# Pairs of a symmetric attention as (i, i + k) mod 128 instead of triangular blocks, with the leaky rectifier in ScalarE's evacuation and the scores put back into rows through DRAM

## The chip, the cores and the metric

One core of one Trainium2 chip. The metric is the device time of one execution in microseconds (us); a kernel's figure is the median of its runs. PE is TensorE, DVE is VectorE, ACT is ScalarE, POOL is GpSimd; hp, ps, d, z and so on are the names of the kernel's tiles: d holds the differences of a tile of pairs, hp their product with W1 (two halves of 64 rows, each a matmul of its own), z the hidden layer behind the leaky rectifier (max(h, 0.01 h), "the leaky" below), ps the scores, lnrs the inverse roots of a layer norm.

## The reference

Four graph layers are applied to 128 batches of 128 tokens with 128 features, all in fp32, each with a layer norm and a maximum with 0 ahead of it and a residual sum behind it. Layer 0 is a relational sum over seven relations. Layers 2 and 3 are plain attention and stay as they were. The change is about layer 1, whose scores come from all pairs of tokens:

```python
D = jnp.abs(x[:, :, None, :] - x[:, None, :, :])        # [128, 128, 128, 128]
h = jnp.einsum('bijc,oc->bijo', D, W1) + b1             # 64 outputs per pair
m = jnp.mean(h, axis=(0, 1, 2))                         # batch norm over every pair of every batch
v = jnp.mean((h - m) ** 2, axis=(0, 1, 2))
h = (h - m) / jnp.sqrt(v + EPS) * g1 + be1
h = _leaky(h)                                           # max(h, 0.01 h)
s = jnp.einsum('bijo,uo->biju', h, W2)[..., 0] + b2[0]
s = jnp.where(A_init > 0, s, NEG)
A = jax.nn.softmax(s, axis=-1)
y = jnp.einsum('bij,bjc->bic', A, x)
# ... linear layer, second batch norm, leaky, concatenation, linear layer
```

D is symmetric, so about half of the pairs suffice. The batch norm needs statistics of all pairs of all batches before any score can be made. The pairs are therefore worked out twice, and the kernel has three stages:

- A: layer 0, woven with the pairs' statistics.
- B: the pairs again, scores, softmax and product of layer 1.
- C: the rest of layer 1, then layers 2 and 3.

## The kernel before

The symmetric half is cut into triangular blocks: block I has rows 16 I to 16 I + 15 and the columns from 16 I on. Five tiles of pairs make a batch.

```python
PAIR_TILES = [(0,), (4,), (2, 6), (1, 7), (3, 5)]
ON_POOL = {(3, 5)}                      # the tile whose differences GpSimd makes
...
def pairwise(pool, xT, blocks):
    n = sum(8 * (P - 16 * I) for I in blocks)
    d = pool.tile([P, 2, 1024], F32, tag="d", bufs=3, name="d")
    ...
    for I in blocks:
        ...
        eng = nc.gpsimd if blocks in ON_POOL else nc.vector
        eng.tensor_tensor(o, <columns of xT>, <rows of xT>, OP.subtract)             # L183
    nc.scalar.activation(d[:, :, :n], d[:, :, :n], AF.Abs)                           # L187
    hp = big("hp").rearrange("p a b -> p (a b)")
    for c in range(0, n, 512):
        for hh in range(2):                                                          # two halves of 64 rows
            nc.tensor.matmul(hp[64 * hh:64 * hh + 64, c:c + 512], w1T,
                             d[:, hh, c:c + 512], start=True, stop=True)             # L191
    return hp, n, places
...
def scores(hT, ps):                                                                  # stage B
    nc.tensor.matmul(ps, ones[0:1, :], b2row, start=True, stop=False, ...)
    for blocks in PAIR_TILES:
        hp, n, places = pairwise(p1, hT, blocks)
        z = p1.tile([P, 1024], F32, name="z")
        nc.scalar.activation(z[:, :n], hp[:, :n], AF.Identity, bias=bias1, scale=scale1[:, 0:1])   # L341
        nc.vector.scalar_tensor_tensor(z[:, :n], z[:, :n], 0.01, z[:, :n],
                                       op0=OP.mult, op1=OP.max)                      # L342, the leaky
        for I, w, off in places:
            for r in range(8):                                                       # 64 small matmuls a batch
                nc.tensor.matmul(ps[q:q + 32, 16 * I:P], w2z[:, s:s + 32],
                                 z[:, off + r * w:off + (r + 1) * w], ...)           # L347
        yield
```

Layer norms take their inverse roots from GpSimd (L136 and L137, tile lnrs), in the same queue as its tile of differences. The input x of all groups of four batches is kept on chip.

## Time and profile before

The median was 7855.92 us (three runs, 7853.16 to 7866.12).

| stage of before | length, us | PE busy | DVE busy | ACT busy |
|---|---|---|---|---|
| A, layer 0 and statistics | 3329 | 69% | 87% | 38% |
| B, scores and softmax | 3081 | 88% | 77% | 61% |
| C, layers 2 and 3 | 1423 | 65% | 64% | 28% |

A stage runs from its own first instruction to the first one of what follows; the batch norms between the stages (some 15 us and 3 us) are in none of them, so that the stretches of the profile lines differ from the table by up to 3 us. Busy shares overlap: in A the DVE is the fullest engine, in B it is PE. The lines themselves stand in the prediction below.

### The profile page before, as it was taken

The numbers are of one execution on the slowest core, as the hardware profiler recorded it, in microseconds if no ns is written. First come the engines' busy times: TensorE is split into PE (matmuls) and PEld (weight loads), VectorE is DVE, ScalarE is ACT, GpSimd is POOL, SyncE is SP. The second block draws the span as 40 slices with busy tenths as digits, with TensorE's granted clock in tenths as the row PEclk, the third lists the DMA queues.
The fourth block names the chain that finished last, engine by engine and source line by source line (L and its number), as shares of the span: only waits on it lengthen the run. The fifth ranks groups of instructions, "written<-read, shape, count | busy, mean of one in ns | idle before, by whom it ended". The sixth has DMA issues, their size and how long they took to land.

```text
span 7851.8 us, 90855 instructions
## 1 busy us (share of the span) xinstructions
PE 5922.0 (75%) x36100; PEld 3189.2 (41%) x36100; DVE 6192.1 (79%) x10853; ACT 3545.3 (45%) x3489; POOL 1368.8 (17%) x884
## 2 busy tenths in 40 slices
PE   6676766777666676688888888888888876666666
PEld 3222222222222222244444444444444445555555
DVE  7888888888888888877777777777777766666666
ACT  2333333333333333355666666666666642222222
POOL 1222222122222222111111111111111210000000
PEclk8777777777777777799999999999999996667666
DMA  2000000000000000000000000000000000000000
GB/s 56 3 3 2 3 3 3 3 3 3 3 3 3 3 2 1 1 1 1 1 1 1 1 1 1 1 1 1 1 1 1 1 2 6 6 9 6 6 6 9
DMA packets 55639, 32.19 MB, mean 4 GB/s; under 512 B 3762, under 2 KB 55218, under 8 KB 55218
## 3 DMA queue, kind: packets, MB, share of 16 engines
q1 hardware_dynamic: 38322, 18.00, 0.9%
q10 hardware_dynamic: 16896, 8.39, 0.3%
q8 instruction: 287, 4.70, 0.2%
q14 instruction: 134, 1.10, 0.0%
HBM read 18.00 MB, written 8.39 MB: 3 GB/s over the span
## 4 chain that ended last, share of the span: by engine, by line
PE 52%; DVE 32%; POOL 7%; ACT 7%; issue 1%; SPq 0%; DMA 0%; POOLq 0%; ACTq 0%; DVEq 0%
PE hp L191 23%; PE ps L347 10%; DVE d L183 9%; ACT d L187 6%; POOL d L183 5%; DVE st_o L210 4%; DVE hn L149 3%; PE pa L264 3%; PE pv L475 3%; PE pa L267 2%; PE ph L258 2%; PE pt L166 2%; DVE z L342 2%; DVE st_d L205 2%; POOL lnrs L137 1%
## 5 line engine op out<-in xcount | busy, mean ns | idle before, releaser
L191 PE MATMUL hp<-d,w1T 128*64 128x512 f32 x9216 | 2906.4, 688 | 854.3 <-ACT d L187 853.2
L187 ACT ACTIVATE d<-d 128x2048 f32<-128x2048 f32 (+1 forms) x1280 | 2192.3, 1734 | 1732.2 <-DVE d L183 1122.9
L183 DVE TENSOR_TENSOR d<-h 128x2048 f32<-128x2048 f32 (+5 forms) x1536 | 2422.0, 1582 | 295.6 <-PE hp L191 295.6
L183 POOL TENSOR_TENSOR d<-h 128x1280 f32<-128x1280 f32 (+1 forms) x512 | 1103.5, 2176 | 4129.6 <-PE hp L191 4118.4
L191 PEld LDWEIGHTS hp<-d,w1T 128*64 128x64 f32 x9216 | 709.0, 151 | 2380.9 <-ACT d L187 1273.0
L347 PE MATMUL ps<-z,w2z 128*32 128x128 f32 (+3 forms) x16384 | 1104.5, 233 | 167.8 <-DVE z L342 167.6
L347 PEld LDWEIGHTS ps<-z,w2z 128*32 128x32 f32 x16384 | 974.8, 112 | 606.3 <-DVE z L342 246.6
L342 DVE SCALAR_TENSOR_TENSOR z<-z 128x1024 f32<-128x1024 f32 (+1 forms) x640 | 963.8, 1511 | 315.7 <-ACT z L341 306.6
L341 ACT ACTIVATE z<-hp,bias,scale 128x1024 f32<-128x1024 f32 (+1 forms) x640 | 714.9, 1117 | 561.9 <-PE hp L191 542.6
L210 DVE BATCH_NORM_STATS2 st_o<-hp 128x6 f32<-128x384 f32 (+5 forms) x1280 | 642.2, 523 | 0.0
L264 PE MATMUL pa<-hw,mask 128*128 128x128 f32 x1792 | 320.6, 320 | 235.2 <-DVE mask L252 184.6
L264 PEld LDWEIGHTS pa<-hw,mask 128*128 128x128 f32 x1792 | 255.8, 214 | 562.8 <-ACT d L187 241.9
L260 ACT COPY hw<-ph 128x384 f32<-128x384 f32 (+1 forms) x256 | 136.3, 533 | 737.1 <-PE ph L258 737.1
L205 DVE BATCH_NORM_STATS2 st_d<-hp 128x6 f32<-128x128 f32 x1024 | 290.6, 289 | 165.0 <-PE hp L191 164.6
L166 PE MATMUL pt<-ident,hn 128*128 128x128 f32 x512 | 138.1, 408 | 367.5 <-DVE hn L160 303.3
L136 POOL TENSOR_SCALAR lnrs<-lnmv 128x4 f32<-128x4 f32 x128 | 30.7, 240 | 1918.2 <-DVE lnmv L144 1918.2
L273 DVE SCALAR_TENSOR_TENSOR o<-pa,rdeg,o 128x128 f32<-128x128 f32 x896 | 300.1, 338 | 11.0 <-PE pa L264 7.1
L166 PE MATMUL pt<-ident,e 128*128 128x128 f32 x640 | 129.0, 355 | 233.2 <-ACT e L459 233.2
L166 PEld LDWEIGHTS pt<-ident,hn 128*128 128x128 f32 x512 | 84.8, 201 | 510.6 <-issue 247.1
L258 PE MATMUL ph<-relw,h 128*128 128x384 f32 (+1 forms) x512 | 283.4, 640 | 0.0
L252 DVE TENSOR_TENSOR mask<-adjT,rel 128x896 f32<-128x896 f32 x128 | 169.5, 1324 | 88.6 <-PE pa L264 88.5
L475 PEld LDWEIGHTS pv<-wr,eT 128*128 128x128 f32 x1280 | 229.6, 280 | 0.0
(143 smaller groups left out, 5161.5 us busy)
## 6 DMA issues: line engine op xcount, KB each, us to landing
x<-in_x_dram SPq DMA_DIRECT2D x32, 256.0 KB, 5.4
adj<-in_adj_dram SPq DMA_DIRECT2D x32, 256.0 KB, 2.8
out_dram<-x ACTq DMA_DIRECT2D x32, 256.0 KB, 2.3
relw<-in_rel_w_dram SPq DMA_DIRECT2D x1, 448.0 KB, 4.3
w<-in_W_dram SPq DMA_DIRECT2D x2, 64.0 KB, 2.1
wgT<-in_WgT_dram SPq DMA_DIRECT2D x1, 64.0 KB, 1.7
wtxT<-in_WtT_dram SPq DMA_DIRECT2D x1, 64.0 KB, 1.8
bt<-in_bt_dram SPq DMA_DIRECT2D x1, 64.0 KB, 3.0
```

Of the source, the lines that this page charges most:

```text
L166: nc.tensor.transpose(pt[:, k, :], src[:, k, :], ident)
L183: eng.tensor_tensor(o, xT[:, None, None, 16 * I:P].to_broadcast([P, 2, 8, w]), rows[:, :, :, None].to_broadcast([P, 2, 8, w]), OP.subtract)
L187: nc.scalar.activation(d[:, :, :n], d[:, :, :n], AF.Abs)
L191: nc.tensor.matmul(hp[64 * hh:64 * hh + 64, c:c + 512], w1T, d[:, hh, c:c + 512], start=True, stop=True)
L205: nc.vector.bn_stats(st_d[:, nd, :], v[:, :, 0:16])
L210: nc.vector.bn_stats(st_o[:, no, :], v[:, r:r + step, 16:])
L258: nc.tensor.matmul(ph[:, 0:r1 - r0, :], hT[:, k, :], relw[:, r0:r1, :], start=True, stop=True)
L264: nc.tensor.matmul(pa[:, r - r0, :], mask[:, r, :], hw[:, r - r0, :], start=True, stop=True)
L341: nc.scalar.activation(z[:, :n], hp[:, :n], AF.Identity, bias=bias1, scale=scale1[:, 0:1])
L342: nc.vector.scalar_tensor_tensor(z[:, :n], z[:, :n], 0.01, z[:, :n], op0=OP.mult, op1=OP.max)
L347: nc.tensor.matmul(ps[q:q + 32, 16 * I:P], w2z[:, s:s + 32], z[:, off + r * w:off + (r + 1) * w], start=False, stop=I % 2 == 1 and r == 7, ...
L475: nc.tensor.matmul(pv[:, k, 0:n], eTs[t][:, k, :], values[t][k], start=True, stop=True)
```

## The change

Pairs are taken as (i, i + k) mod 128 for k = 1 to 64. All tiles are then alike: four of 2 x 8 x 128 pairs for a batch. Almost every DVE, ACT and PE instruction on the pairs has its full 512, 1024 or 2048 columns (the statistics of a batch's last tile have 384 and 128), and there are 16 hp matmuls a batch in place of 18. The leaky moves into the evacuation on ACT (Prelu with slope 0.01), so DVE loses one instruction per tile. Eight 512-column ps matmuls replace 64 small ones. Scores come out by k; they are picked into columns (pk), stored to DRAM along skewed rows, and loaded back as rows. To pay for the room, x lives in DRAM. GpSimd still makes one tile of differences of each batch, now one of four, and also copies h into the extended tile xe.

The core of the diff (comments, constants and the tail of the softmax are cut):

```diff
-PAIR_TILES = [(0,), (4,), (2, 6), (1, 7), (3, 5)]
-ON_POOL = {(3, 5)}
+KH = 32
+KC = 8
+ROW = P + 2 * KH
+ON_POOL = {1}
...
-    X = [res.tile([P, G, P], F32, tag=f"x{g}", name=f"x{g}") for g in range(NG)]
+    X = [dr.tile([P, G, P], F32, tag=f"x{g}", name=f"x{g}") for g in range(NG)]      # dr is in DRAM
...
-    def pairwise(pool, xT, blocks):
+    def around(pool, hT):
+        xe = pool.tile([P, G, P + 2 * KH], F32, name="xe")
+        nc.gpsimd.tensor_copy(xe[:, :, 0:P], hT)
+        nc.gpsimd.tensor_copy(xe[:, :, P:], hT[:, :, 0:2 * KH])
+        return xe
+
+    def pairwise(pool, xe, k, t):
+        d = pool.tile([P, 2, KC, P], F32, tag="d", bufs=3, name="d")
+        x = xe[:, k, 0:P]
+        ahead = ...                                    # xe from 1 + KC * t on, KC windows in each half
+        eng = nc.gpsimd if t in ON_POOL else nc.vector
+        eng.tensor_tensor(d, ahead, x[:, None, None, :].to_broadcast([P, 2, KC, P]), OP.subtract)
...
-            _weave(pairs(g), layer0(g + 1) if g + 1 < NG else iter(()), 3)
+            _weave(pairs(g), layer0(g + 1) if g + 1 < NG else iter(()), 4)
...
-                nc.scalar.activation(z[:, :n], hp[:, :n], AF.Identity, bias=bias1, scale=scale1[:, 0:1])
-                nc.vector.scalar_tensor_tensor(z[:, :n], z[:, :n], 0.01, z[:, :n], op0=OP.mult, op1=OP.max)
-                for I, w, off in places:               # 64 small matmuls
+                nc.scalar.activation(z, hp, AF.Prelu, bias=bias1, scale=scale1[:, 0:1], alpha=0.01)
+                for c in range(2):
+                    j = 2 * t + c
+                    q, w = 32 * (j % 4), 31 - 2 * (j // 4)
+                    nc.tensor.matmul(ps[q:q + 32, :], w2z[:, w:w + 32], z[:, 512 * c:512 * c + 512],
+                                     start=j < 4, stop=j >= 4, skip_group_check=True)
...
+            nc.sync.dma_start(bass.AP(..., ap=[[ROW + 1, P], [P * ROW, G], [1, 1 + 2 * KH]]), s)
+            u = p1.tile([P, G, ROW], F32, name="u")
+            nc.sync.dma_start(u, rows.rearrange("g i r -> i g r"))
```

## The prediction

> **What bounds the kernel now.** I read first the busy time by stretches, cut where the code changes stage (columns: stretch, its length, then busy us and instruction count of PE, PE weight loads, DVE, ACT and POOL, the granted PE clock, DMA share, GB/s):
>
> ```profile
> 0.00:75.00 75.00, 30.16 (x158) 22.05 (x160) 34.44 (x106) 9.72 (x15) 9.51 (x26) 0.84 0.54 139
> 75.00:3329.00 3254.00, 2261.42 (x9188) 921.53 (x9188) 2858.31 (x5887) 1259.88 (x979) 705.02 (x470) 0.78 0.01 3
> 3344.00:6428.00 3084.00, 2703.19 (x22070) 1492.03 (x22066) 2376.92 (x2455) 1877.47 (x1821) 571.15 (x258) 0.96 0.00 1
> 6428.00:7851.00 1423.00, 921.54 (x4672) 750.71 (x4672) 910.11 (x2379) 393.44 (x672) 82.36 (x128) 0.69 0.02 7
> ```
>
> Stage A (to 3329: layer 0 woven with the pairs' statistics) keeps DVE 88% busy, PE 69% at a clock of 0.78. Stage B (to 6428: layer 1's scores and softmax) keeps PE 88% busy at 0.96, DVE 77%. Stage C (layers 2 and 3) fills nobody. Per batch, A takes 3254/127 = 25.6 us with 22.5 of DVE, B 3084/128 = 24.1 us with 21.1 of PE.
>
> Who waits in A confirms DVE: the first two lines are ACT waiting for DVE and PE for that ACT, while DVE's largest wait for PE is small.
>
> ```profile
> ACT d L187 <- DVE d L183: 1099.2, 319, 8.2
> PE hp L191 <- ACT d L187: 641.8, 229, 8.2
> DVE st_d L205 <- PE hp L191: 164.6, 255, 4.5
> ```
>
> In B, one batch of the chain that ended last shows mostly PE, plus one hole per batch in which the POOL tile is made and then rectified:
>
> ```profile
> 4984.24 1.02 PE hp L191 x2
> ...
> 4985.42 4.21 POOL d L183 x2
> 4989.65 3.72 ACT d L187 x2
> ...
> 4993.41 3.65 PE hp L191 x14
> 4997.06 1.64 PE ps L347 x28
> 4998.70 1.00 PE hp L191 x2
> ```
>
> The durations I use come from the groups kept apart by shape (busy us, mean ns; an fp32 matmul is two instructions):
>
> ```profile
> L187 ACT ACTIVATE d<-d 128x2048 f32<-128x2048 f32 x1024 | 1921.3, 1903 | 1599.4 <-DVE d L183 1070.4 <-POOL d L183 525.1 <-PE hp L191 4.0
> L341 ACT ACTIVATE z<-hp,bias,scale 128x1024 f32<-128x1024 f32 x512 | 615.5, 1202 | 513.0 <-PE hp L191 495.6 <-PE ps L347 17.4
> L183 DVE TENSOR_TENSOR d<-h 128x2048 f32<-128x2048 f32 x256 | 584.3, 2282 | 99.5 <-PE hp L191 99.5
> L183 DVE TENSOR_TENSOR d<-h 128x512 f32<-128x512 f32 x256 | 300.6, 1174 | 0.0
> L210 DVE BATCH_NORM_STATS2 st_o<-hp 128x6 f32<-128x384 f32 x384 | 200.4, 550 | 0.0
> L210 DVE BATCH_NORM_STATS2 st_o<-hp 128x6 f32<-128x512 f32 x128 | 87.4, 683 | 0.0
> ```
>
> **What the Trainium skill says.** (1) "TensorE: Matmul & The Clock Gate", rules for kernel authors, small-M row: outputs in distinct column groups run at the same time. The trace agrees: eight hp instructions (four matmuls, both halves in turn) take 1.92 us on the chain, whereas the two instructions of a single matmul, issued without its partner, take 1.00. (2) "TensorEngine Tiling (Array Packing)", key properties: changing the tiling mode drains the array. hp uses 64 columns, ps 32, so a half left alone before ps matmuls should not overlap them; the 1.00 us above, followed by ps at once, agrees. (3) "ScalarE: Activation LUTs": every function costs the same per element, but another table set costs a reload. Abs and Identity fit one slope here; before has one table load, and the built program after also has just one, so Prelu shares the set with Exp. (4) "SBUF — State Buffer", who interferes with whom: a DVE instruction with two SBUF inputs contends with a GpSimd instruction that reads SBUF. The 512-element d above takes 1174 ns in the mean where other DVE operations of 512 elements take about 690, so it does.
>
> **Stage A, part by part.** Pairs fall from 18 to 16 matmuls and from 9216 to 8192 columns per batch. DVE per batch now: statistics L210 392/78 = 5.0, L205 177.5/78 = 2.3, two aggregates 0.7, in all 8.0 us. After: seven of 512 columns (7 x 0.683 = 4.8), one of 384 (0.55), one of 128 (0.28), aggregates of about 0.5: 6.1. Saved 1.9. Differences on DVE now: 745.7/78 = 9.6 us, of which about 1.2 is waiting for POOL's port (the 512 and 256 forms take 1174 and 886 ns instead of some 690 and 410). After: three of 2048, 6.8 us, and I keep the 1.2: 8.0. Saved 1.5. POOL still makes 2048 columns per batch, plus the copies into xe. So DVE goes from 22.5 to 19.1 us; with the idle 3.1 us per batch kept, a batch takes 22.2, and A becomes 127 x 22.2 + 75 = 2895 us. PE falls by 2/18 of its 11.4 us of hp, so it doesn't become the bound (17.8 - 1.3 = 16.5). The x store and loads are 256 KB each, two buffers deep, and out-transfers of this size land in 2.3 us: hidden.
>
> **Stage B.** DVE loses the leaky operation (630 us in a window of 2000 us that holds 83.3 batches: 7.6 us per batch) and the softmax becomes one instruction per group. DVE after: 3 x 2.28 for d, 0.69 for the copy of ps, 0.4 for the two small ones, and a group's twelve or so 512-column instructions at 0.42 to 0.69 (8.7 us) over four: 10.1 us, from 19. DVE is out of the way. ACT: four Abs of 1.90, four Prelu of 1.20, and 2.5/4 for the rest: 13.0 us, from 15 (614.9 per 1000 us).
>
> PE decides. Now hp is 935.7/83.3 = 11.2 us and ps 719.4/83.3 = 8.6 us. A whole pair of halves costs 2 x 0.427 = 0.85 us (1.92 for two pairs less start-up). I counted in the built order: before, 356 of 1152 pairs are split by other work between the halves; after, 350 of 1020, which is 2.74 per batch. Check on before: (9 + 2.8) x 0.853 + 4.5 starts x 0.15 = 10.8, measured 11.2, ratio 1.04, which fits the clock of 0.96. After: (8 + 2.74) x 0.853 + 5 x 0.15 = 9.9, times 1.04 = 10.3. ps: 64 small matmuls per batch become 8 of 512 columns in four column groups, issued two at a time in 3.75 runs: 3.75 x (0.853 + 0.15) x 1.04 = 3.9, from 8.6. New: four pk products with 16 columns, bound like the 1-column L267 (14 instructions in 1.46 us on the chain), eight instructions, about 1.1 us. Transposes and the linear layers by group: 1.24, from 2.2 with the bias product. Sum 16.6 us, from 21.1.
>
> So PE still bounds B, 3.6 us above ACT. Idle beside PE was 3.0 us per batch, mostly the POOL hole; POOL still makes one 2048-column tile (4.2 us), followed by one Abs instead of two, with a little more room in the ring of three d buffers relative to its tile. I take 1.2 us of idle: 17.8 us, 2278 for the stage. The scores' trip through DRAM (store, load, some 5 us by the 2.3 us landings) comes once a group on DVE, which has 7 us of slack a batch: mostly hidden.
>
> **Stage C.** Same work. x must be loaded; three buffers with two groups in flight means that every second group waits for an out-transfer and a load, about 3 us of which DVE has no other work, x16, and hn with one buffer adds under 1 us x32: 1423 + 60 = 1485.
>
> **Sum.** 2895 + 25 (between stages) + 2278 + 1485 = 6683, I say 6690 us, 0.85 of before.
>
> **Rivals.** (a) The split pairs cost less than a whole pair each, or the POOL hole closes and PE follows ACT: B at 15.5 us, total about 6390. For: ACT alone is 13.0, and the ps column groups could fill beside a lone half. Against: the 1.00 us steps on the chain. (b) New coupling: ACT now has both Abs and Prelu in one strict order with PE, and DVE stands in order behind a DRAM round trip; B at 20 us, total about 6970. For: the hole of 8 us on the chain arises in just this way. Against: ACT and DVE both have slack. (c) In A, PE becomes the bound: its clock is 0.78, and hp ran twice as long in cold stretches; then A gains only PE's 1.3 us: A 3160, total about 6950. Against: DVE hardly waits for PE in A. (d) ACT's Prelu switches table sets against Exp: at 1.3 us a load, twice a group, only 80 us; excluded by the build.
>
> **Range.** B and A are each good to about 200 us, C to 40; together some 300 either way at 8 in 10, with rivals (a) and (b) as the ends: 6380 to 7030. Slower than before by over 2% would need every saving to be eaten by coupling; I give 1%, and 2% for within 2%.
>
> **What would show it.** Right: A near 2900 us with DVE at 85% or more; B near 2280 with PE above 90% busy, hp near 10 and ps near 4 us a batch, ACT near 13; C near 1480 with a wait for the DMA of x. Wrong: PE in B well under 85% busy with ACT or a DMA as its releaser (then rival b), ps not running in parallel, Prelu over 1.2 us, a clock in B under 0.9, or DVE under 80% busy in A.

## The result, and the profile after

The changed kernel took 6773.84 us in the median (four runs, 6772.93 to 6787.43), beside 7854.54 us for the kernel before on the same chip. The ratio is 0.8626, with a 95% interval from 0.8613 to 0.8638. Ratios here are the mean time of one kernel's runs over that of the kernel before in the same rounds, so they are not quite the ratio of the medians.

The total is 1.3% above the predicted 6690 us. The stages show that this closeness owes something to luck:

| stage | before | predicted | after | after minus predicted |
|---|---|---|---|---|
| A | 3329 | 2895 | 3226 | +331 |
| B | 3081 | 2278 | 2113 | -165 |
| C | 1423 | 1485 | 1429 | -56 |

The stretches of A and B in the changed kernel, with the columns that the prediction explains (busy us and instructions of PE, PE weight loads, DVE, ACT and POOL, then the granted PE clock, DMA share, GB/s):

```profile
75.00:3225.00 3150.00, 2188.44 (x8688) 969.34 (x8688) 2427.42 (x4382) 1139.99 (x855) 862.64 (x415) 0.79 0.03 8
3240.00:5353.00 2113.00, 1931.94 (x7986) 611.80 (x7986) 1353.43 (x1307) 1587.21 (x1149) 578.30 (x187) 0.99 0.06 17
```

**A.** DVE's work fell as predicted, from 2858 to 2427 us: 2427 over 127 batches is 19.1 us each. But the stretch shrank by only 104 us. DVE now idles 3150 - 2427 = 723 us, where it idled 3254 - 2858 = 396. The waits of DVE in A say on what, in us in total, times, longest; first the kernel before:

```profile
DVE mask L252 <- PE pa L264: 88.5, 31, 3.3
DVE hn L149 <- POOL lnrs L137: 44.3, 30, 1.5
DVE rdeg L269 <- PE pa L267: 35.0, 61, 2.0
```

and the kernel after:

```profile
DVE st L203 <- PE hp L193: 229.6, 223, 4.7
DVE hn L148 <- POOL lnrs L136: 158.7, 31, 5.2
DVE rdeg L266 <- PE pa L264: 158.1, 124, 2.4
DVE mask L249 <- PE pa L261: 104.7, 62, 2.2
```

Before, the wait for hp was 164.6 us (it is among the prediction's lines). The four growths are 65, 114, 123 and 16 us: 318 of the 327 us of added idle. One is a wait for GpSimd, three are waits for PE.

The chain of waits in A shows what the wait for GpSimd is made of, once a group of four batches (start us, us, what):

```profile
1543.54 4.22 POOL xe L175
1547.76 0.34 POOL xe L176
1548.10 4.15 POOL d L187
1552.27 3.72 ACT d L189 x2
1556.03 6.52 PE hp L193 x16
```

The timeline of DVE over the same time has the other end of it:

```profile
1553.59 1.11 DVE L148 TENSOR_SCALAR hn<-x,lnmv,lnrs 128x128 f32<-128x128 f32 x4 [5.24 <-POOL lnrs L136]
```

The copies into xe and GpSimd's d run first in its queue, and the inverse root of the next group's layer norm stands behind them. DVE, which all of layer 0 goes through, waits 5.24 us for one small instruction, and PE starts its next 16 hp instructions only at 1556. The copy's 4.22 us are not all its own: its mean is 3.94 us in A and 0.68 in B, and here two of DVE's d tiles (4.48 us from 1542.81) run at the same time. So DVE also holds up GpSimd, and then waits for it.

**B.** Groups of B kept apart by shape (busy us, mean ns, then the engine's idle time before them):

```profile
L193 PE MATMUL hp<-d,w1T 128*64 128x512 f32 x4080 | 1218.1, 610 | 1.2 <-ACT d L189 1.2
L187 DVE TENSOR_TENSOR d<-xe 128x2048 f32<-128x2048 f32 x380 | 914.4, 2407 | 478.1 <-PE hp L193 475.5
L372 ACT ACTIVATE z<-hp,bias,scale 128x1024 f32<-128x1024 f32 x512 | 608.4, 1200 | 352.9 <-PE hp L193 352.7
L187 POOL TENSOR_TENSOR d<-xe 128x2048 f32<-128x2048 f32 x127 | 545.5, 4295 | 1275.8 <-PE hp L193 1247.4 <-ACT d L189 28.4
L376 PE MATMUL ps<-z,w2z 128*32 128x512 f32 x2048 | 508.4, 608 | 93.3 <-ACT z L372 93.3
L406 DVE TENSOR_TENSOR u<-u 128x256 f32<-128x256 f32 x32 | 79.6, 2487 | 53.5 <-DMA u<-rows 53.5
```

The Prelu costs 1200 ns, as the Identity of before did (1202). The trip of the scores through DRAM shows as 53.5 us of waiting in the whole stage, and C is 6 us longer with x from DRAM. PE is busy 1932 of 2113 us at a clock of 0.99. Some of what idles it is still GpSimd's tile, as one batch of the chain shows:

```profile
4426.68 4.60 POOL d L187
4431.30 1.92 ACT d L189
```

### The profile page after: what moved, and what is told of

Read it like the earlier page. It is cut to its first block, busy times and chain, and to the rows that moved or that the text cites. A ratio compares the mean times of both kernels' runs of the same rounds, so it can differ in the third digit from the quotient of the medians.

```text
span 6785.6 us, 58156 instructions
## 1 busy us (share of the span) xinstructions
PE 5091.2 (75%) x21510; PEld 2364.6 (35%) x21510; DVE 4731.7 (70%) x8187; ACT 3135.1 (46%) x2690; POOL 1536.1 (23%) x754
## 4 chain that ended last, share of the span: by engine, by line
PE 45%; DVE 30%; POOL 11%; ACT 9%; issue 4%; DMA 0%; SPq 0%; POOLq 0%; DVEq 0%; ACTq 0%
PE hp L193 20%; DVE d L187 9%; POOL d L187 6%; ACT d L189 5%; PE ps L376 5%; PE pa L264 3%; PE pv L526 3%; PE pa L261 3%; PE pt L165 3%; PE ph L255 2%; ACT z L372 2%; DVE st L203 2%; POOL xe L175 2%; DVE st L205 2%; PE pk L383 2%
## 5 line engine op out<-in xcount | busy, mean ns | idle before, releaser
L193 PE MATMUL hp<-d,w1T 128*64 128x512 f32 x8192 | 2553.4, 684 | 673.0 <-ACT d L189 541.7
L189 ACT ACTIVATE d<-d 128x2048 f32<-128x2048 f32 x1024 | 1938.8, 1906 | 935.6 <-POOL d L187 451.2
L187 DVE TENSOR_TENSOR d<-xe 128x2048 f32<-128x2048 f32 x768 | 1964.2, 2561 | 479.7 <-PE hp L193 477.1
L187 POOL TENSOR_TENSOR d<-xe 128x2048 f32<-128x2048 f32 x256 | 1096.6, 4284 | 3036.2 <-PE hp L193 3007.7
L372 ACT ACTIVATE z<-hp,bias,scale 128x1024 f32<-128x1024 f32 x512 | 608.4, 1200 | 352.9 <-PE hp L193 352.7
L376 PE MATMUL ps<-z,w2z 128*32 128x512 f32 x2048 | 508.4, 608 | 93.3 <-ACT z L372 93.3
L203 DVE BATCH_NORM_STATS2 st<-hp 128x6 f32<-128x512 f32 x512 | 352.7, 689 | 229.6 <-PE hp L193 229.6
L205 DVE BATCH_NORM_STATS2 st<-hp 128x6 f32<-128x512 f32 (+1 forms) x512 | 332.3, 649 | 0.0
L264 PEld LDWEIGHTS pa<-ones,mask 128*128 128x128 f32 x1792 | 259.0, 229 | 0.0
L264 PE MATMUL pa<-ones,mask 128*128 128x1 f32 x1792 | 252.8, 270 | 0.0
```

Of the source, the lines that this page charges most:

```text
L187: eng.tensor_tensor(d, ahead, x[:, None, None, :].to_broadcast([P, 2, KC, P]), OP.subtract)
L189: nc.scalar.activation(d, d, AF.Abs)
L193: nc.tensor.matmul(hp[64 * hh:64 * hh + 64, c:c + 512], w1T, d[:, hh, c:c + 512], start=True, stop=True)
L203: nc.vector.bn_stats(st[:, 2 * t, :], hp[:, 0:512])
L205: nc.vector.bn_stats(st[:, 2 * t + 1, :], hp[:, 512:1024 - P * last])
L264: nc.tensor.matmul(pa[:, 3, r:r + 1], mask[:, r, :], ones[:, 0:1], start=True, stop=True)
```

## The experiments

Two questions were open. Why did A keep so little of DVE's saved work? My theory was GpSimd's tile, with its late delivery and its hold on memory access; the rivals were a DVE that is still the plain bound, and the copies into xe alone. And what did B gain from: the leaky on ACT, the shape of the pairs, or both? Twelve kernels ran. Those without a ratio ran once: their state is unknown, and their stage lengths are read from a profile. Stage lengths are given as A / B; C was between 1425 and 1431 us in all of them.

### The leaky on ACT alone, in the kernel before

```diff
-nc.scalar.activation(z[:, :n], hp[:, :n], AF.Identity, bias=bias1, scale=scale1[:, 0:1])
-nc.vector.scalar_tensor_tensor(z[:, :n], z[:, :n], 0.01, z[:, :n], op0=OP.mult, op1=OP.max)
+nc.scalar.activation(z[:, :n], hp[:, :n], AF.Prelu, bias=bias1, scale=scale1[:, 0:1], alpha=0.01)
```

> The kernel before, with the leaky part alone moved into the ACT evacuation (Prelu in place of Identity, the DVE max of z removed). Stages A and C should not move (3329 and 1423 us). In stage B, 7.6 us of DVE work per batch goes, and 1.2 us of latency between hp and ps for each tile. Theory (B was bound by PE, 21.1 of 24.1 us per batch busy): B falls only by part of PE's idle 3.0 us, 0.5 to 1.5 us per batch, that is 60 to 200 us; total 7650 to 7790 us. Rival (the leaky operation was the main reason why B got 970 us faster): B falls by over 400 us, total under 7450.

Measured: 7886.56 us, ratio 1.0033 (1.0018 to 1.0048); stages 3325 / 3113. My expectation of a gain fell.

```profile
3340.00:6453.00 3113.00, 2740.74 (x22070) 1444.21 (x22066) 1744.73 (x1810) 1868.49 (x1822) 572.36 (x256) 0.95 0.00 1
```

DVE lost 632 us of work in B, and the stage became 32 us longer. PE was busy 2741 us against 2703 and idle for 372 against 381. It was not that PE had no wait for the leaky. One of its waits in B before, and one with the edit:

```profile
PE ps L347 <- DVE z L342: 167.6, 156, 4.1
PE pat L377 <- DVE u L375: 207.4, 128, 2.1
```

PE's waits for z and for d fell from 168 and 205 us to 38 and 113, by 221 in all. But a wait that had been 2 us became 207: a transpose of each batch's softmax (pat) now waited for DVE's u. One wait took the place of others. What puts u later in this order was not tested.

### The leaky back on DVE, in the kernel after

```diff
-nc.scalar.activation(z, hp, AF.Prelu, bias=bias1, scale=scale1[:, 0:1], alpha=0.01)
+nc.scalar.activation(z, hp, AF.Identity, bias=bias1, scale=scale1[:, 0:1])
+nc.vector.scalar_tensor_tensor(z, z, 0.01, z, op0=OP.mult, op1=OP.max)
```

> The kernel after, with the leaky part put back on DVE (Identity on ACT, then z max 0.01 z on DVE). DVE in B goes from 10.6 to about 15.5 us per batch plus waits for POOL's port, just under PE's 15.1 busy of 16.5. Theory: there is little slack left beside PE, so B lengthens by 1 to 3 us per batch, 130 to 400 us, total 6900 to 7170 us, all in B. Rival (PE alone decides): B within 60 us of 2113, total 6770 to 6840.

Measured: 7483.33 us, ratio 0.9519 (0.9504 to 0.9535); stages 3225 / 2814. The same edit that was worth nothing in the old kernel costs 701 us here, more than I expected. The stretch of B, and the wait that names it:

```profile
3240.00:6054.00 2814.00, 2207.06 (x7986) 664.97 (x7986) 2264.53 (x1816) 1597.51 (x1148) 647.40 (x187) 0.86 0.04 13
PE ps L377 <- DVE z L373: 496.0, 193, 4.4
```

PE's idle time grew by 426 us (181 to 607), and 496 of the 607 are this wait. Its busy time grew by 275 us for the same 7986 instructions, at a granted clock of 0.86 in place of 0.99. Whether the waits lowered the clock was not tested.

### No tile of differences on GpSimd, in the kernel after

```diff
-ON_POOL = {1}
+ON_POOL = set()
```

> The kernel after, with all differences on DVE and none on POOL. In B DVE has slack: the 4.2 us of POOL on the chain go, and B falls by 0.5 to 1.3 us per batch (60 to 170 us). In A it depends. If A is bound by DVE's work, DVE does 20 us per batch in place of 19 and A grows by about 130 us (to 3350). If A's shortfall comes from what queues on POOL (the inverse roots of the norms behind a 4.2 us difference, the copies into xe that hold up the port), DVE's waits for the norms vanish and A stays or falls, by up to 150 us (3075 to 3225).

Measured: 6408.49 us, ratio 0.8153 (0.8141 to 0.8165); stages 2953 / 2007. DVE gets a third more differences to make (four tiles a batch in place of three), and both stages are faster, A by more than the 150 us that I had allowed for.

```profile
75.00:2953.00 2878.00, 2052.05 (x8662) 875.78 (x8662) 2484.84 (x4480) 1152.26 (x850) 359.88 (x280) 0.86 0.03 9
2968.00:4975.00 2007.00, 1897.73 (x7986) 595.82 (x7986) 1510.93 (x1431) 1592.29 (x1148) 92.21 (x60) 0.99 0.06 18
```

In A, DVE's idle time falls from 723 to 2878 - 2485 = 393 us, what it was in the kernel before. Its busy time rises by only 57 us, though the 127 tiles that it took over cost 2.28 us each, 290 us by themselves: most of the rest came back because its d tiles fell from 2.71 to 2.28 us in the mean (0.43 us on 386 tiles are 167 us). Of its other instructions only the normalising of o changed clearly (0.54 to 0.34 us). Its waits change by -115 (inverse roots, to 44.2), -82 (rdeg, to 75.9), -105 (mask, to none), -71 (st, to 158.6) and +46 (o for the roots, to 85.5). So GpSimd's tile, whose purpose is to spare DVE, costs 273 us in A and 106 in B.

### The same, in the kernel before

```diff
-ON_POOL = {(3, 5)}
+ON_POOL = set()
```

> The kernel before, with POOL's tile of differences on DVE. If A of before is bound by DVE's work and POOL's tile is a real help there, A grows by about 1 us per batch, 130 us (3330 to 3460). If POOL's tile costs more than it saves in general, and not only in the kernel after, A falls by over 100 us as it did after. In B the hole behind POOL (4.2 us and two Abs) goes: 1.5 to 2.5 us per batch, B at 2760 to 2890 with PE over 93% busy.

Measured: 7523.47 us, ratio 0.9576 (0.956 to 0.9592); stages 3187 / 2887. GpSimd's tile was a loss in the old kernel too, of 142 us in A and 194 in B, where PE was 89% busy and not over 93% as I had expected. This was no fault that the change brought in; the change made the loss in A about twice as large.

### The copies into xe on ACT, GpSimd's tile kept

```diff
-nc.gpsimd.tensor_copy(xe[:, :, 0:P], hT)
-nc.gpsimd.tensor_copy(xe[:, :, P:], hT[:, :, 0:2 * KH])
+nc.scalar.copy(xe[:, :, 0:P], hT)
+nc.scalar.copy(xe[:, :, P:], hT[:, :, 0:2 * KH])
```

> The kernel after, with the copies into xe on ACT in place of POOL; POOL keeps its tile of differences. In A the group's boundary has, one after the other, a copy of 4.2 us on POOL (mean 3.9, held up by DVE's port), POOL's difference of 4.2 us, and only then the inverse roots that DVE waits 5 us for. If xe is a large part of A's lost 330 us, A falls by 60 to 150 us (to 3075 to 3165). If POOL's difference alone is to blame, A falls by under 30 us. B within 30 us of 2113, C unchanged.

Measured: 6813.12 us, ratio 0.8668 (0.8655 to 0.8681); stages 3149 / 2220. In A the wait for the inverse roots falls from 158.7 to 44.2 us, and the stage gains 77: the copies are a part of A's loss, not most of it. B, which I had expected within 30 us, loses 107, with PE's busy time 96 us up at a clock of 0.97 instead of 0.99. DVE's busy time rose there by 165 us for the same work (its d tiles took 2.55 us in the mean instead of 2.41, its norms of h 1.24 instead of 0.40). Why it did was not settled; the edit is no gain.

### Four buffers for d, GpSimd's tile kept

```diff
-d = pool.tile([P, 2, KC, P], F32, tag="d", bufs=3, name="d")
+d = pool.tile([P, 2, KC, P], F32, tag="d", bufs=4, name="d")
```

> The changed kernel with four buffers for the differences d in place of three; GpSimd keeps its tile. Theory (GpSimd delivers one tile of each group late, 4.2 us, and a ring of three leaves TensorE and VectorE no slack to ride it out): the stage of layer 0 falls from 3226 by 100 to 250 us. Rival (what costs is VectorE's access to memory taken by GpSimd, and the inverse roots and copies that queue behind its d): a further buffer gives under 60 us in layer 0.

Measured: 6569.15 us (one run); stages 3111 / 2005.

```profile
75.00:3111.00 3036.00, 2112.50 (x8684) 907.63 (x8684) 2515.83 (x4359) 1136.28 (x854) 931.23 (x410) 0.84 0.03 8
3129.00:5134.00 2005.00, 1940.45 (x7986) 593.80 (x7986) 1418.05 (x1305) 1592.66 (x1146) 592.05 (x186) 0.99 0.06 18
```

In B the kernel with GpSimd's tile comes level with the one without: 2005 us against 2007, and PE's idle time falls from 181 to 65 us. (A fourth buffer without GpSimd's tile was not run, so what the tile costs with four stays open.) There the fault was the ring of three, in which a tile that takes 4.3 us holds up those behind it. In A the gain is 115 of the 273 us, within the theory's range but near its low end. The idle time of DVE falls to 520 us, and its busy time rises by 88, for the same work. One more buffer hides the late tile, not the time that the two engines take from each other.

### Less statistics on DVE (a wrong result by intent)

```diff
             nc.vector.bn_stats(st[:, 2 * t, :], hp[:, 0:512])
             last = t == KH // KC - 1
-            nc.vector.bn_stats(st[:, 2 * t + 1, :], hp[:, 512:1024 - P * last])
             if last:
+                nc.vector.bn_stats(st[:, 2 * t + 1, :], hp[:, 512:1024 - P * last])
                 nc.vector.bn_stats(st[:, 8, :], hp[:, 1024 - P:])
-        nc.vector.bn_aggr(ST1[:, b, 0, :], st.rearrange("p a b -> p (a b)"))
+        nc.vector.bn_aggr(ST1[:, b, 0, :], st[:, 6:8, :].rearrange("p a b -> p (a b)"))
```

> A wrong result on purpose. The kernel after, with the statistics of the second half of the first three tiles of each batch left out in stage A: DVE does 3 x 0.63 us = 1.9 us less per batch and nothing else changes. If A is bound by DVE's work as the prediction had it, A falls by 1.9 x 127 = 240 us (at least 180). If A is now bound by a chain of waits through POOL, PE and ACT, A falls by under 100 us. B and C don't move (2113 and 1432).

Measured: 6488.91 us, ratio 0.8255 (0.8242 to 0.8267); stages 2915 / 2110.

```profile
75.00:2915.00 2840.00, 2060.97 (x8676) 900.23 (x8675) 2291.91 (x3969) 1142.58 (x852) 851.66 (x407) 0.86 0.03 9
```

Statistics of a part of the pairs were near enough for the comparison to pass, but this is not the reference's sum. A falls by 311 us, more than the work that was removed. DVE's busy time fell by 136 us (2427 to 2292) and its idle time by 175. The rival that A is a pure chain, where DVE's work doesn't count, falls. But the idle time isn't a fixed sum per batch either, as my prediction had it: the wait for inverse roots fell from 158.7 to 29.4 us, though nothing on GpSimd was changed (the copy into xe, 3.94 us in the mean before, took 1.57). It depends on how the engines' queues happen to meet.

### The two halves of hp apart

```diff
-for c in range(0, KC * P, 512):
-    for hh in range(2):
+for hh in range(2):
+    for c in range(0, KC * P, 512):
```

> The kernel after, with the two loops around hp's matmuls exchanged: both columns' chunks of half 0 first, then those of half 1. The same four matmuls, no pair next to each other. If two halves overlap only when they are neighbours in PE's order, hp takes up to 16 x 0.85 us = 13.6 us per batch in B in place of 9.6 and B grows by 3 to 4.5 us per batch, 380 to 570 us; A grows too, by 100 to 400 us. If PE overlaps them at any distance of a few instructions, B stays within 60 us.

Measured: 6958.11 us (one run); stages 3212 / 2299. In B hp takes 1341 us instead of 1218, which over 127.5 batches (4080 instructions, 32 a batch) is 10.5 us instead of 9.6. Had all overlap of the two halves been lost, B would have grown by 380 us or more; it grew by 186, and A did not grow at all, against what I expected. PE's instructions of B in this trace, counted in runs between other work of PE, show when halves overlap. All four matmuls of a tile (8 instructions) with nothing else between took 1.94 us (211 runs), as long as with neighbouring pairs in the runs below: there the distance costs nothing. Two of them alone (4 instructions, 156 runs) took 1.93 us, as long as all four: across other work there was no overlap.

### Whole pairs: hp at high priority, no tile on GpSimd

```diff
-ON_POOL = {1}
+ON_POOL = set()
...
+        with tc.high_priority():
             for c in range(0, KC * P, 512):
                 for hh in range(2):
                     nc.tensor.matmul(hp[...], w1T, d[:, hh, c:c + 512], start=True, stop=True)
```

> The kernel after without POOL's tile (so beside e3_after_no_pool: A 2953, B 2007), and hp's matmuls traced at a higher priority, which in the built order leaves not one pair split (350 of 1020 were). If a split pair costs a second pass of 0.85 us, hp falls in B from 9.7 to about 7.8 us per batch; PE then needs about 13.2 and ACT 12.4, so B comes to 13.8 to 14.8 us per batch, 1770 to 1890 us. If splits cost little, B stays within 40 us of 2007. In A only 93 of 1028 pairs were split: within 60 us of 2953.

Measured: 6336.35 us, ratio 0.8063 (0.8051 to 0.8075); stages 3104 / 1784. In the built order no pair of B is split, where 350 of 1020 were. B gains 223 us over the kernel without GpSimd's tile. hp takes 7.8 us a batch instead of 9.4. But A loses 150 us:

```profile
DVE rdeg L267 <- PE pa L265: 230.3, 121, 3.0
```

This wait was 75.9 us with the scheduler's own order. With hp always first, layer 0's small matmuls come late, and DVE waits for them. But PE's busy time in A also rose, from 2052 to 2186 us, at a clock of 0.79 instead of 0.86; the two effects were not separated.

### The same in B only

```diff
-    def pairwise(pool, xe, k, t):
+    def pairwise(pool, xe, k, t, first=False):
...
+        with tc.high_priority() if first else nullcontext():
...
-                hp = pairwise(p1, xe, k, t)                 # in scores, stage B
+                hp = pairwise(p1, xe, k, t, first=True)
```

> The changed kernel without GpSimd's tile, and the product matmuls (hp) of the scores stage alone put at high priority, so that no pair of halves is split there (0 split pairs in the built order) while the stage of layer 0 keeps the scheduler's own order. Theory (the 223 us that whole pairs saved in the scores and the 150 us that the order cost in layer 0 are separate effects of order in each stage): stage of layer 0 2953 us (within 60), scores 1784 us (1750 to 1830), layers 2 and 3 1430, total about 6180 (6130 to 6250). Rival (the 150 us of layer 0 came from another arrangement, not from its order): layer 0 stays at 3050 or more, total about 6300.

Measured: 6192.64 us, ratio 0.7887 (0.7874 to 0.79); stages 2956 / 1784. Both effects add as the theory had it, and this is the fastest kernel: 8.6% less time than the changed kernel by the two medians.

```profile
2972.00:4756.00 1784.00, 1732.17 (x7986) 547.89 (x7986) 1507.42 (x1432) 1563.55 (x1147) 30.78 (x60) 0.99 0.07 20
```

PE is busy 97% of B, ACT 88%, DVE 84%. The chain of B is now mostly whole groups of PE:

```profile
4001.65 0.98 PE ps L377 x4
...
4003.68 1.87 PE hp L194 x8
...
4019.24 0.97 PE ps L377 x2
```

Two ps matmuls (four instructions) take 0.98 us here, and one alone takes 0.97: the column groups of ps run beside each other.

### The two corners left: leaky on DVE or on ACT, without GpSimd's tile

In the kernel after, without GpSimd's tile, with the leaky back on DVE:

```diff
-ON_POOL = {1}
+ON_POOL = set()
...
-nc.scalar.activation(z, hp, AF.Prelu, bias=bias1, scale=scale1[:, 0:1], alpha=0.01)
+nc.scalar.activation(z, hp, AF.Identity, bias=bias1, scale=scale1[:, 0:1])
+nc.vector.scalar_tensor_tensor(z, z, 0.01, z, op0=OP.mult, op1=OP.max)
```

> The changed kernel without GpSimd's tile and with the leaky of the scores' hidden layer put back on VectorE. Theory (the 701 us that the leaky on VectorE cost is VectorE's own work and its order: d, maximum and scores' reductions in one queue of about 17 us a batch): the scores stage stays at 2400 us or more, against 2007 without that edit. Rival (GpSimd's d blocks VectorE's maximum, and without it the queue flows): scores at 2100 to 2260 us.

Measured: 6906.68 us (one run); stages 2959 / 2498. The leaky on DVE still costs 491 us when GpSimd makes no differences. So 491 of the 701 stay without GpSimd's tile, which I put down to DVE's own work and place in the order, and some 210 came with the tile: the leaky took 1.62 us in the mean beside it and 1.23 without, and the clock of B was 0.86 beside it and 0.93 without.

In the kernel before, without GpSimd's tile, with the leaky on ACT:

```diff
-ON_POOL = {(3, 5)}
+ON_POOL = set()
...
-nc.scalar.activation(z[:, :n], hp[:, :n], AF.Identity, bias=bias1, scale=scale1[:, 0:1])
-nc.vector.scalar_tensor_tensor(z[:, :n], z[:, :n], 0.01, z[:, :n], op0=OP.mult, op1=OP.max)
+nc.scalar.activation(z[:, :n], hp[:, :n], AF.Prelu, bias=bias1, scale=scale1[:, 0:1], alpha=0.01)
```

> The kernel before, without GpSimd's tile and with the leaky in ScalarE's evacuation: the last corner of blocks or pairs, GpSimd or not, leaky on VectorE or ScalarE. Theory (the old blocks leave TensorE as the bound of the scores stage whatever is taken from VectorE): scores within 100 us of the 2887 of the same kernel with the leaky on VectorE. Rival (VectorE's and GpSimd's delays were both hiding the gain of the leaky): scores fall by more than 200, to under 2690.

Measured: 7435.03 us (one run); stages 3197 / 2792. With GpSimd out of the way the leaky on ACT gains 95 us in the old kernel, just inside the theory's bound of 100. PE is 91% busy there.

Length of B in us, all eight corners:

| pairs | leaky on DVE, tile on GpSimd | leaky on ACT, tile on GpSimd | leaky on DVE, no tile | leaky on ACT, no tile |
|---|---|---|---|---|
| triangular blocks | 3081 | 3113 | 2887 | 2792 |
| (i, i + k) | 2814 | 2113 | 2498 | 2007 |

The two parts of the change don't add up. With GpSimd's tile, new pairs alone give -267, the leaky alone +32, both together -968. PE's and DVE's busy times in B give the direction. With blocks PE needs 21.1 us a batch and DVE 18.6 with the leaky, so relieving DVE alone can gain at most PE's 3.0 us of idle time, and the waits that moved left nothing of that. With the new pairs PE needs 15.1 (1932 over 128 batches), and DVE with the leaky 17.7 (2265 over 128 in the run with the leaky back; 16.4 without GpSimd's tile, where PE needs 16.1). Then DVE is the longer one, and relieving it lets B come down towards PE. The sums don't give the size: B took 22.0 and 19.5 us a batch in the two runs with the leaky on DVE, more than either engine's sum there (PE 17.2 and 16.1), because PE also waits for the leaky in its turn. Nor was it tested how much the new kernel owes to doing its softmax once a group, so that it has no transpose of each batch to wait for.

## Why the prediction was right or wrong

The total was right, by errors that cancel: A was 331 us too low, B and C together 221 too high.

- **The bounds (DVE in A, PE in B).** Right for B: PE is 91% busy, as announced, and the fastest version brings it to 97%. In A DVE's work matters, as the run with fewer statistics shows, but DVE was 77% busy, below the 80% that I had named as a sign of being wrong.
- **A, DVE's work at 19.1 us a batch.** Right: 19.1.
- **A, "with the idle 3.1 us per batch kept": this step failed.** DVE's idle time became 723 / 127 = 5.7 us a batch. The 2.6 us more, over 127 batches, are the whole error of A. I treated idle time as a constant that an edit of the work leaves alone. It is the outcome of queues meeting. Without GpSimd's tile A takes 2953 us with 393 us of idle time, close to the predicted 2895 and 396; so what the step left out comes with the tile. Its parts: the wait for inverse roots queued behind it and the held-up copy (115 us by the waits), its slow delivery into a ring of three (115 us by the fourth buffer; in part the same time, because that run also lost the wait for inverse roots), and waits for PE's products. How the remainder divides between the hold on memory access and the order on PE stays open. So does the clock: it was 0.79 in A and 0.86 without the tile, with PE busy 2188 and 2052 us. It doesn't go with the tile alone (0.86 in the run with fewer statistics, which keeps the tile, and 0.79 in the one with hp first in both stages, which has none), and these runs can't tell whether it is cause or effect.
- **A, rival (c), PE as the bound with A at 3160.** Close in the number, not shown as the reason. DVE does wait for PE more (492 us in the lines above, 288 before), but an edit that leaves PE's work alone and takes the tile off GpSimd removes 258 us of those waits. That edit raised the clock too, so what a slower PE has in it isn't excluded.
- **B, "a split pair costs a whole pair".** Mis-sized. hp was 9.6 us a batch, not 10.3. By the two kernels without GpSimd's tile, with 2.74 split pairs a batch and with none, the split costs (9.4 - 7.8) / 2.74 = 0.58 us each, not 0.85 (both traces of B with the scheduler's order show 350 of 1020 pairs split, those with hp first show none). Put at one pass for each 0.85 us of its runs of hp, PE spent an estimated 9.3 passes a batch in the changed kernel, where whole pairs take 8 and one more for every split pair would make 10.7; so cut-off halves of different pairs often ran as one. The rest of B's error is PE's sum: the groups of hp, ps, pk and the linear layers add up to 15.7 us a batch, of which 0.6 overlap, where I had 16.6.
- **B, ps at 3.9, pk at 1.1, 1.2 us of idle time.** Right: 4.0, 1.05 and 1.4. Rival (a) was half true, and rival (b) didn't occur: the Prelu costs ACT nothing extra, and DVE waited 0.4 us a batch for the DRAM trip.
- **B, which part gains.** The prediction added the parts up engine by engine and took the longest, which is the right way to do it; it said that the leaky takes DVE "out of the way", and the corners confirm that it is needed. That alone it would be worth nothing, I had not seen: my expectations for both one-part runs were off.
- **C, 60 us for x from DRAM.** Wrong in size: 6 us at most, since the three edited versions of the kernel before, with x on chip, had 1427 us in C too. Three buffers were enough.

## What to carry to other kernels

Work out each engine's time per step with all parts of a change together: an edit that relieves the second-longest engine can gain no more than the idle time of the longest, and even that can go to a wait that moves (the leaky alone gave +32 us); once the longest has come down, the same edit can gain most of all. A slice given to a slower engine is no free help: try it without, and with one more buffer, because its late tile and its hold on memory can cost the fast engine more than the slice saved. Look at the order of the built program as well as at its counts: a priority on one group of matmuls gained 223 us in one stage and went with a loss of 150 in another, so give it by stage.

## What the Trainium skill lacked or had wrong

- "GPSIMD Engine Reference", introduction, calls GpSimd the wrong choice for ordinary elementwise work because VectorE is roughly twice as fast; the trace agrees (4.30 us a tile on GpSimd in B, 2.28 on VectorE in the runs without GpSimd's tile). "SBUF — State Buffer", in its summary, advises to schedule whichever of the two is off the critical path. Neither says that such an offload can be a net loss even where VectorE is the fullest engine: without it this kernel was 365 us faster and the one before 331. Nor do they say that the number of buffers has a part in it: a fourth d buffer brought B from 2113 to 2005 us, against 2007 without the offload, and won 115 of 273 us in A.
- "ScalarE: Activation LUTs", section on what each stage is for, names Parametric ReLU and then says "None of it is reachable from a kernel today". Read as being about the function, that misleads: Prelu with alpha 0.01 ran with right results, at 1200 ns for 1024 columns (1202 for Identity). No page lists it beside Exp in one table set, though the kernel with both has a single table load.
- "TensorE: Matmul & The Clock Gate", section "Why this matters for your kernels", small-M row: it gives a speedup for matmuls in distinct column groups, and no price for partners that are apart. Here partners apart with nothing between them overlapped as neighbours do (four matmuls in 1.94 us), two cut off from their partners by other work took as long as four (1.93), pairs split by other work cost 0.58 us each, and whole pairs throughout gave hp 7.8 us a batch.
- "TensorEngine Tiling (Array Packing)", key properties, says that a change of tiling mode drains the array, and gives no time for it. No run here measured that drain by itself; a lone half ahead of ps took 1.00 us on the chain.
